# Scaled sums and column sums moved between engines, exponentials in a pool of their own, and the first work of the next stage in another order

## The chip, the core and the metric

The kernel runs on one core of a Trainium2 chip. The metric is the device time of one execution in microseconds (us). An engine is named here as the profile names it: PE is the matrix engine (PEld its weight loads), ACT is ScalarE, DVE is VectorE, POOL is GpSimd, SP is SyncE, which only issues transfers. The queues of ACT and SP both carry DMA issues.

## The reference

The input `x` is 4 images of 128 channels and 64 x 64 points, in float32. Two layers follow one another.

```python
# layer 0: convolutions of 7x7, 5x5 and 3x3 and a full attention over the 4096 points of an image
v = gn(x)
x7, x5, x3 = conv2d(v, w7, b7, 3), conv2d(v, w5, b5, 2), conv2d(v, w3, b3, 1)
f = einsum('bcn,bcm->bnm', theta(v), phi(v)) / sqrt(64)
xn = conv1x1(einsum('bcm,bnm->bcn', g(v), softmax(f)), ow, ob) + v
x = x + relu(x7 + x5 + x3 + xn + v)
# layer 1: a two-way Mamba layer over the 4096 tokens of an image, then a recurrence
t = tokens(x)
t = t + mamba(ln(t), fwd) + reverse(mamba(reverse(ln(t)), bwd))
t = t + scan(lambda y, w: sigmoid(w + y @ V.T), batch_norm(ln(t) @ W.T))
```

In `mamba` a token is projected to z, x, B, C and dt; x, B and C pass a causal filter of four taps and a silu; then comes a scan over chunks, whose decays are exponentials of differences of cumulated dt.

## The kernel before

One program holds three stages, `conv_attention` (0 to about 1711 us of the profile), `mamba` and `recurrence`. A fallback in plain forms follows under an `If`, which is not entered with these inputs. The images lie side by side in one tile `t` for the whole program: 128 channels x 4 x 4096 points.

**Steps.** `conv_attention` runs 32 steps: 4 images (b) by 8 (q). A step does two things at once. The first is the attention of 512 query points over the 4096 keys of the image, in 8 iterations of the loop `for i in range(NB)`. An iteration has `scores` for the iteration after it (8 matmuls L453 into `pf`, two exponentials L455 into `ex`) and `values` (8 matmuls L464 from `ex` into `acc`, and two sums of exponentials on DVE into `es`, the first of a step on L468, the others on L470). `ex` is a tag with four buffers, of which an iteration takes two. At the end of the step L639 folds `es`, and `divide` takes its column sums with a matmul (`den`, L474).

The second is one of eight parts, called m, of the joint convolution. All three kernels are summed into one 7x7 kernel, and the rows of the image are convolved in a transformed domain (groups of output rows j = 0 to 3, with transformation points U and V and their squares UU and VV), which needs fewer products. `transform` (L292 to L325) and `forms` (L335 to 344) make the transformed rows `yx`, `yd`, `yf` of part m on ACT and POOL during the attention iterations. `convolve` then runs the products (`products`, L364) between the attention of this step and that of the next. The parts of an image are done in the orders

```python
        FIRST = (6, 7, 1, 2, 0, 5, 3, 4)
        ORDER = (1, 2, 0, 6, 7, 5, 3, 4)
        LAST = (1, 2, 3, 4, 6, 7, 5, 0)
```

for image 0, for images 1 and 2, and for image 3.

**Adding into the image.** Every part's result `eo` has to be added to some of the four output rows j. `put` does that. The first contribution to a place (kept in `begun`) is a copy on POOL, or a multiply on ACT where it is scaled. Later ones are an add on POOL (L387) or, where scaled, two scalar_tensor_tensor on DVE (L390). The parts 1 and 2, and likewise 3 and 4, belong together: sum and difference of the two (L423, L424, L429) go to j = 0, 2 and to j = 1, 3 with factors. These scaled contributions are not put at once. `later` appends them to the list `late`, and one is taken off in each attention iteration of the following step. So they fall in the step after m = 2 and in the step after m = 4. For which of them a place is already begun depends on the order of the parts.

**Weights.** `weights` is a generator that is advanced once per iteration in the first two steps. It sums the three kernels (`sums`, L534), makes sums and differences of the kernel's columns (`thirds`, L542 to L544, in each of the two `SLOT`s), and then the transformed weights (`pair`, L571 to L575, and `store`, L564), which go to DRAM as `wd`. From there `fetch` (L369, on ACT's queue) brings the weights of a part: two of its three tiles in iteration NB-2 of its step, the third in `convolve`. The tag `wt` has two buffers.

**Mamba's start.** `mamba` loads both in-projections (`full_fwd`, `full_bwd`, on SP's queue) and the filter taps (`cw_fwd`, `cw_bwd`, on ACT's), and the scales of the normalization for every token (`tl`, from `first`, on SP's queue). `centre` (L118, L119) takes the mean off the in-projections; `scaled` (L907) multiplies `tl` by the tokens. Then `project_bc`, `project` (L1106 to L1117: the backward x and half of the forward x, a matmul and the filter's taps on ACT and DVE), `project_fwd` (L1097: the other half, filtered in four matmuls), `activate` (silu, L1121) and `differences` (eight subtractions L1150 into `lt`, followed later by an exponential on L1173) prepare the first chunk.

**What sets the order of the work.** On PE and ACT the instructions stand in the order of the program (`manual_schedule`). On DVE, POOL and SP a scheduler orders them from the dependencies and its own estimates, so that the same source line can be placed in front of or behind other work of the step. Tiles are given out by pools: memory of a pool that has been closed is given to a later one, and a load into it waits for the last use of what lay there. The tiles `ex`, `xn` (the normalized image of `keys`) and `es` are in pool `l0_wk`, and so are `eo`, `mid`, `u`, `xr`, `att` and the small ones.

Of the kernel before, what the change touches and what calls it, by code (L numbers as in the profile page):

```python
# [10 lines left out]
F32 = mybir.dt.float32  # L11
AF = mybir.ActivationFunctionType
ALU = mybir.AluOpType
# [140 lines left out]
def conv_attention(nc, tc, k, a, t, B, H, W, flags, load, mem, loads):  # L154
# [32 lines left out]
    with ExitStack() as ctx:  # L187
# [26 lines left out]
        for i, name in enumerate(("b7", "b5", "b3", "ob")):  # L214
            nc.sync.dma_start(bias[:, i : i + 1], a[name])
        nc.gpsimd.memset(xp, 0.0)
        wk = ctx.enter_context(tc.tile_pool(name="l0_wk", bufs=2))
        big = ctx.enter_context(tc.tile_pool(name="l0_big", bufs=1))
        dram = ctx.enter_context(tc.tile_pool(name="l0_dram", bufs=1, space=bass.MemoryType.DRAM))
# [36 lines left out]

        def keys(b, j):

            xn = wk.tile([P, XT // P, P], F32, tag="ex", name="xn", bufs=4)
            nc.vector.tensor_scalar(  # L260
                xn.rearrange("p a l -> p (a l)"), t[:, ds(b * T + j * XT, XT)], *gn[b], ALU.subtract, ALU.mult
            )
            pp = ps_c.tile([P, NC], F32, tag="c", name="pp")
            for e in range(2):
                nc.tensor.matmul(pp[HALF[e]], pw, xn[:, e::2, :], start=True, stop=True)
            n = XT // P
            nc.scalar.activation(
                phi[:, ds(j * n // 2, n // 2), :].rearrange("p a l -> p (a l)"), pp, AF.Identity, bias=pb2
            )
            pg = ps_c.tile([P, NC], F32, tag="c", name="pg")  # L270
            for e in range(2):
                nc.tensor.matmul(pg[HALF[e]], gw, xn[:, e::2, :], start=True, stop=True)
            g = wk.tile([P, NC], F32, tag="row", name="g", bufs=1)
            nc.scalar.copy(g, pg)
            yield
            pt = ps_c.tile([P, n // 2, 2, IC], F32, tag="c", name="gt")
            for i in range(n // 2):
                nc.tensor.transpose(pt[:, i].rearrange("p e c -> p (e c)"), g[:, bass.ts(i, P)], k.ident)
            nc.scalar.copy(gT[:, ds(j * n, n), :], pt.rearrange("p i e c -> p (i e) c"))
# [92 lines left out]
        def convolve(b, m, f, wts):  # L372

            image = t[:, b * T : (b + 1) * T].rearrange("p (k g j c x) -> p g j x k c", g=2, j=4, c=PC, x=2)
            in_ = lambda v: v.rearrange("p x (k c) -> p x k c", c=PC)

            def put(n, j, v, by=1.0):

                out = image[:, n - 1, j]
                if (b, n, j) not in begun:  # L380
                    begun.add((b, n, j))
                    if by == 1.0:
                        nc.gpsimd.tensor_copy(out, v)
                    else:
                        nc.scalar.mul(out, v, by)
                elif by == 1.0:
                    nc.gpsimd.tensor_tensor(out, out, v, ALU.add)  # L387
                else:
                    for x in range(2):
                        nc.vector.scalar_tensor_tensor(out[:, x], v[:, x], by, out[:, x], ALU.mult, ALU.add)  # L390

            by = BY.get(m, 1.0)
            base = None
            for n in range(3):
                if f[n] is None:
                    continue
                fn = [v + (u,) for v, u in zip(f[n], (wts[n], wc) if wts else (wc,))]
                pm = products(fn, (1, 2))
                keep = n and m in (1, 3)
                eo = wk.tile([P, 2, KB // 2 * PC], F32, tag=f"mid{n}" if keep else "eo", name="eo", bufs=1 if keep else 4)  # L400
                nc.scalar.mul(eo[:, 1, :], pm[:, 1, :], by / 2)  # L401
                if wts and n == 1:
                    wts.append(fetch(m, 2))
                for e, op in enumerate((ALU.add, ALU.subtract)):
                    nc.vector.scalar_tensor_tensor(eo[:, e, :], pm[:, 0, :], by / 2, eo[:, 1, :], ALU.mult, op)  # L405
                yield
                pm = products(fn, (0, 3))
                if by == 1.0:
                    nc.vector.tensor_tensor(eo, eo, pm, ALU.add)  # L409
                else:  # L410
                    nc.vector.scalar_tensor_tensor(eo, pm, by, eo, ALU.mult, ALU.add)  # L411
                if n == 0:
                    base = eo
                    yield
                    continue
                if m < 6:
                    nc.gpsimd.tensor_tensor(eo, eo, base, ALU.add)  # L417
                if keep:
                    mid[n] = eo
                elif m == 2:  # L420
                    begun.add((b, n, 0))
                    out = image[:, n - 1, 0]
                    nc.gpsimd.tensor_tensor(out, in_(mid[n]), in_(eo), ALU.add)  # L423
                    nc.gpsimd.tensor_tensor(mid[n], mid[n], eo, ALU.subtract)  # L424
                    for j, v, c in ((2, out, UU), (1, in_(mid[n]), U), (3, in_(mid[n]), U * UU)):
                        later(put, n, j, v, c)
                elif m == 4:
                    u = wk.tile([P, 2, KB // 2 * PC], F32, tag="u", name="u", bufs=2)
                    nc.gpsimd.tensor_tensor(u, mid[n], eo, ALU.add)  # L429
                    nc.gpsimd.tensor_tensor(mid[n], mid[n], eo, ALU.subtract)  # L430
                    put(n, 0, in_(u))
                    for j, v, c in ((2, u, VV), (1, mid[n], V), (3, mid[n], V * VV)):
                        later(put, n, j, in_(v), c)
                else:
                    put(n, {0: 0, 5: 3, 6: 1, 7: 2}[m], in_(eo))
                yield
# [10 lines left out]
        def scores(th, m0):  # L447

            out = []
            for m in range(2 * m0, 2 * m0 + 2):  # L450
                pf = ps_f.tile([P, 2, NC], F32, tag="f", name="pf")
                for e in range(2):
                    nc.tensor.matmul(pf[:, e, :], phi[HALF[e], m, :], th[HALF[e]], start=True, stop=True)  # L453
                ex = wk.tile([P, 2, NC], F32, tag="ex", name="ex", bufs=4)
                nc.scalar.activation(ex, pf, AF.Exp, scale=scale)  # L455
                out.append(ex)
            return out
# [41 lines left out]
        def later(f, *args):  # L499

            late.append(lambda: f(*args))
# [17 lines left out]
        def weights():  # L519
# [18 lines left out]
            def thirds(y0, y1, s):  # L538

                v, new = [w[:, y0:y1, s[i], :] for i in (0, 1, 3)], w[:, y0:y1, s[2], :]  # L540
                ac = free[:, 25 : 25 + y1 - y0, :] if y1 - y0 == 1 else free[:, 0 : y1 - y0, :]
                nc.vector.tensor_tensor(ac, v[0], v[2], ALU.add)  # L542
                nc.gpsimd.tensor_tensor(new, ac, v[1], ALU.subtract)
                nc.vector.tensor_tensor(v[1], ac, v[1], ALU.add)  # L544

            sums(3, 4)

# [65 lines left out]
        for n in range(N):  # L613
# [10 lines left out]
            if more:  # L624
                rows(b + 1, 0, H)
            acc = ps_v.tile([P, NC], F32, tag="v", name="acc")
            es = wk.tile([P, 2, NC], F32, tag="es", name="es", bufs=1)
            for i in range(NB):
                exs = nxt
                if i + 1 < NB:  # L630
                    nxt = scores(th, i + 1)
                values(i, exs, acc, es)
                next(making_forms, None)
                next(making, None)
                if m < 6 and i == NB - 2:
                    wts = [fetch(m, 0), fetch(m, 1)]
                if late:
                    late.pop(0)()
# [231 lines left out]
def mamba(nc, tc, k, a, t, B, T, vec, first=None, after=None, mr=None):  # L870
# [16 lines left out]
    with ExitStack() as ctx:  # L887
# [204 lines left out]
        def project_fwd(gr):  # L1092

            tl, g = gr["tl"], gr["at"][1]
            px = ring.tile([P, MG], F32, tag="big", name="px")
            for tap in range(KC):
                nc.tensor.matmul(px, w[0]["x"][:, tap, :], tl[:, rows(g, 0, tap)], start=(tap == 0), stop=(tap == KC - 1))  # L1097
            nc.scalar.activation(gr["x"][0][:, 0, :], px, AF.Silu, bias=w[0]["cb"][:, 0:1])
# [46 lines left out]
        def differences(m):  # L1145

            for d in range(ND):
                for h in range(NHEAD):
                    v = m["lt"][:, d, h, :]
                    nc.scalar.activation(v, v, AF.Relu, scale=-1.0, bias=m["b"]["cs"][:, d, m["i"], h : h + 1])  # L1150
# [224 lines left out]
        open_step(1)  # L1375
        for act in later:
            act()
        for i, c in STEPS_X:
            project(groups[0], i, c)
        project_fwd(groups[0])  # L1380
        for i, c in STEPS_X:
            activate(groups[0], i, c)
        differences(m[0])
        turn(m[0])
        prepare(m[0])
        differences(m[1])
# [349 lines left out]
```

## Time and profile before

| | us |
|---|---|
| median of 3 runs | 3203.11 |
| lowest and highest run | 3199.3, 3203.25 |
| the profiled execution | 3203.28 |
| its span, first to last instruction | 3201.6 |
| of that, `conv_attention` | about 1711 |
| PE busy | 2957.4 |
| DVE, POOL, ACT busy | 2288.2, 1824.4, 1803.1 |

The mean clock that PE was granted is 0.973 of full speed.

How lines of the profile read: a group is a source line, an engine, an operation, `out<-in` by the names of tiles, shape and count; then the busy time in us and the mean of one in ns; then how long the engine stood idle just before such instructions, and what ended most of that. A line of the waits is the waiting engine and instruction, then `<-` the instruction that released it, and in us the total, the number and the longest. A line of a timeline is the start in us from the beginning of the span, the duration of a run of like instructions, and in brackets the idle time before it. `L` numbers are lines of the kernel before.

### The profile page before, as it was taken

To read this page: it belongs to the slowest core of one execution; us is meant where nothing else is said; L and a number is where in the kernel's file an instruction comes from. 1 tells how busy PE (TensorE), PEld (TensorE's weight loads), DVE (VectorE), ACT (ScalarE), POOL (GpSimd) and SP (SyncE) were. 2 spreads that over 40 slices of the span, in tenths; PEclk is the share of its full clock that TensorE was granted. 3 is DMA by queue.
4 is the path that set the end of the run, shared out by engine and by line. 5 is a ranking of instruction groups with operands and counts; after the bars stand their busy time and mean duration, and the time that the engine had idled before them with its cause. 6 is when DMAs were issued, how large, how long until landed. Compare 5 with 4: busy or idle time off the path is not lost. (4 is left out here: it accounts for less than half of the span.)

```text
span 3201.6 us, 42877 instructions
## 1 busy us (share of the span) xinstructions
PE 2957.4 (92%) x15511; PEld 1463.9 (46%) x15511; DVE 2288.2 (71%) x3476; ACT 1803.1 (56%) x3074; POOL 1824.4 (57%) x1375
## 2 busy tenths in 40 slices
PE   6899999999999999899997899999999999999976
PEld 1344443545444453434443454544444544445445
DVE  6886778767878568687675676767676767777667
ACT  3333434344344334353442887887788778888756
POOL 5166757817668257596073355556655665556644
PEclk9899999999999999999998899999999999999988
DMA  5310010200102001010004233333433444343332
GB/s 190 126 38 30 23 45 23 71 1 23 39 29 66 7 23 38 30 57 30 1 25 130 73 106 107 90 97 84 115 97 93 93 110 97 97 99 93 87 113 107
DMA packets 108393, 224.15 MB, mean 70 GB/s; under 512 B 25678, under 2 KB 29390, under 8 KB 106764
## 3 DMA queue, kind: packets, MB, share of 16 engines
q1 hardware_dynamic: 96588, 177.53, 19.8%
q10 hardware_dynamic: 11584, 43.78, 4.0%
q8 instruction: 125, 2.05, 0.3%
q14 instruction: 96, 0.79, 0.1%
HBM read 200.83 MB, written 20.44 MB: 69 GB/s over the span
## 5 line engine op out<-in xcount | busy, mean ns | idle before, releaser
L470 DVE TENSOR_TENSOR es<-es,ex 128x1024 f32<-128x1024 f32 x448 | 730.5, 1630 | 108.2 <-ACT ex L455 69.5
L455 ACT ACTIVATE ex<-pf 128x1024 f32<-128x1024 f32 x512 | 501.2, 1023 | 479.1 <-PE pf L453 371.8
L453 PE MATMUL pf<-theta,phi 64*128 64x512 f32 x2048 | 524.1, 630 | 49.0 <-ACT ex L455 47.5
L464 PE MATMUL acc<-ex,gT 128*64 128x512 f32 x2048 | 493.5, 608 | 4.5 <-ACT ex L455 4.5
L1184 POOL TENSOR_TENSOR ct<-ct,Cst 128x512 f32<-128x512 f32 x128 | 170.5, 1332 | 397.3 <-DMA ct<-csmem 335.5
L453 PEld LDWEIGHTS pf<-theta,phi 64*128 64x128 f32 x2048 | 175.1, 189 | 374.8 <-ACT ex L455 237.5
L1150 ACT ACTIVATE lt<-lt,cs 128x128 f32<-128x128 f32 x1024 | 312.1, 390 | 0.0
L364 PE MATMUL pm<-yf,wt 128*128 128x256 f32 x1152 | 286.6, 381 | 21.5 <-DMA wt<-wd 20.5
L401 ACT ACTIVATE eo<-pm 128x256 f32<-128x256 f32 x88 | 33.8, 384 | 476.2 <-PE pm L364 461.5
L464 PEld LDWEIGHTS acc<-ex,gT 128*64 128x64 f32 x2048 | 127.7, 137 | 346.0 <-issue 331.7
L364 PEld LDWEIGHTS pm<-yf,wt 128*128 128x128 f32 x1152 | 212.3, 189 | 97.7 <-issue 44.9
L335 POOL TENSOR_TENSOR yf<-yd 128x272 f32<-128x272 f32 x192 | 253.0, 1349 | 0.0
L1085 PE MATMUL pb<-tl,wbc_fwd 128*64 128x512 f32 x512 | 236.0, 604 | 1.9 <-DVE xT L1117 1.9
L1085 PE MATMUL pb<-tl,wbc_bwd 128*64 128x512 f32 x512 | 236.6, 604 | 0.0
L417 POOL TENSOR_TENSOR eo<-eo 128x512 f32<-128x512 f32 x48 | 61.6, 1284 | 272.7 <-DVE eo L411 190.1
L1249 POOL TENSOR_TENSOR yT<-yT,zT 128x512 f32<-128x512 f32 x127 | 168.3, 1334 | 33.7 <-DVE yT L1236 31.4
L1183 DVE TENSOR_TENSOR lt<-lt,gm 128x1024 f32<-128x1024 f32 x128 | 181.7, 1420 | 1.9
L387 POOL TENSOR_TENSOR t<-t,eo 128x512 f32<-128x512 f32 x28 | 38.0, 1356 | 226.9 <-DVE eo L409 225.7
L335 POOL TENSOR_TENSOR yf<-yx 128x272 f32<-128x272 f32 x96 | 149.9, 1590 | 1.9
L1117 DVE SCALAR_TENSOR_TENSOR xT<-px,taps_bwd,xT 128x512 f32<-128x512 f32 x192 | 143.7, 749 | 8.1 <-ACT xT L1111 3.3
L1216 PE MATMUL y<-lt,xdt 128*64 128x128 f32 x2048 | 141.8, 281 | 7.8 <-PE ptr L1159 4.0
L405 DVE SCALAR_TENSOR_TENSOR eo<-pm,eo 128x256 f32<-128x256 f32 x176 | 73.5, 418 | 101.4 <-ACT eo L401 99.2
(295 smaller groups left out, 5794.3 us busy)
## 6 DMA issues: line engine op xcount, KB each, us to landing
lt<-csmem SPq DMA_DIRECT2D x128, 512.0 KB, 5.6
wt<-wd ACTq DMA_DIRECT2D x72, 576.0 KB, 3.8
ct<-csmem SPq DMA_DIRECT2D x256, 128.0 KB, 5.3
rs<-m SPq DMA_DIRECT2D x31, 512.0 KB, 3.8
wd<-t SPq DMA_DIRECT2D x16, 576.0 KB, 2.8
t<-in_x SPq DMA_DIRECT2D x4, 2048.0 KB
rows<-after SPq DMA_DIRECT2D x32, 256.0 KB, 4.5
out<-t SPq DMA_DIRECT2D x4, 2048.0 KB, 14.4
```

Of the source, the lines that this page charges most:

```text
L335: nc.gpsimd.tensor_tensor(f[:, kx], at(x), at(y), op)
L364: nc.tensor.matmul(pm[:, e, :], wt, src, start=(i == 0), stop=(i == len(terms) - 1))
L453: nc.tensor.matmul(pf[:, e, :], phi[HALF[e], m, :], th[HALF[e]], start=True, stop=True)
L455: nc.scalar.activation(ex, pf, AF.Exp, scale=scale)
L464: nc.tensor.matmul(acc[HALF[e]], gT[:, 2 * m + e, :], ex[:, e, :], start=(m == 0), stop=(m == NT // 2 - 1))
L470: nc.vector.tensor_tensor(es, es, ex, ALU.add)
L1085: nc.tensor.matmul(out, w[i]["bc"][:, tap, bass.ts(c, DS)], src, start=(tap == 0), stop=(tap == KC - 1),)
L1117: nc.vector.scalar_tensor_tensor(at(n), px, taps[:, PAD - n : KC - n], at(n), ALU.mult, ALU.add)
L1150: nc.scalar.activation(v, v, AF.Relu, scale=-1.0, bias=m["b"]["cs"][:, d, m["i"], h : h + 1])
L1183: nc.vector.tensor_tensor(lt, lt, gm.unsqueeze(2).to_broadcast([P, ND, NHEAD, P]), ALU.mult)
L1184: nc.gpsimd.tensor_tensor(m["ct"], m["ct"], Cs[:, cols].unsqueeze(1).to_broadcast([P, NHEAD, P]), ALU.mult)
L1249: eng.tensor_tensor(v, v, gr["z"][d][:, :, half(d, j // 2)], ALU.mult)
```

## The change

Five things differ.

1. `ex`, `xn` and `es` get a pool of their own, `l0_ex`, opened before `l0_wk`. The memory that `mamba` gives to the in-projections and the taps is then that of the exponentials.
2. In `put`, a scaled contribution is multiplied on ACT: into the image where it is the first, else into a tile. That tile is a spare of tag `xr` (two buffers), or, for j = 3, the result itself in place. The add is one instruction on POOL. The scheduled contributions are appended by the new `put_middle`, in the same order j = 2, 1, 3.
3. The two DVE sums of `thirds` go to POOL, where the third operation already was.
4. The first two weights of a part are fetched in iteration NB-3 instead of NB-2.
5. At Mamba's start `project_fwd` comes before the `project`s, and `differences` between these and `activate`. The same order is in the fallback.

The line numbers of the new kernel are higher by 2 from L216 on and by 5 from about L430 on.

```diff
+        ep = ctx.enter_context(tc.tile_pool(name="l0_ex", bufs=4))
         wk = ctx.enter_context(tc.tile_pool(name="l0_wk", bufs=2))
...
-            xn = wk.tile([P, XT // P, P], F32, tag="ex", name="xn", bufs=4)
+            xn = ep.tile([P, XT // P, P], F32, tag="ex", name="xn")
...
-            def put(n, j, v, by=1.0):
+            def put(n, j, v, by=1.0, own=None):
 
                 out = image[:, n - 1, j]
-                if (b, n, j) not in begun:
-                    begun.add((b, n, j))
-                    if by == 1.0:
-                        nc.gpsimd.tensor_copy(out, v)
-                    else:
-                        nc.scalar.mul(out, v, by)
+                if by != 1.0:
+                    to = out if (b, n, j) not in begun else in_(own)
+                    nc.scalar.mul(to, v, by)
+                    v = to
+                if (b, n, j) in begun:
+                    nc.gpsimd.tensor_tensor(out, out, v, ALU.add)
                 elif by == 1.0:
-                    nc.gpsimd.tensor_tensor(out, out, v, ALU.add)
-                else:
-                    for x in range(2):
-                        nc.vector.scalar_tensor_tensor(out[:, x], v[:, x], by, out[:, x], ALU.mult, ALU.add)
+                    nc.gpsimd.tensor_copy(out, v)
+                begun.add((b, n, j))
+
+            def put_middle(n, u, v, at):
+
+                spare = lambda: wk.tile([P, 2, KB // 2 * PC], F32, tag="xr", name="sc")
+                later(lambda: put(n, 2, u, at * at, spare() if (b, n, 2) in begun else None))
+                later(lambda: put(n, 1, in_(v), at, spare() if (b, n, 1) in begun else None))
+                later(lambda: put(n, 3, in_(v), at * at * at, v))
...
-                    for j, v, c in ((2, out, UU), (1, in_(mid[n]), U), (3, in_(mid[n]), U * UU)):
-                        later(put, n, j, v, c)
+                    put_middle(n, out, mid[n], U)
...
-                    for j, v, c in ((2, u, VV), (1, mid[n], V), (3, mid[n], V * VV)):
-                        later(put, n, j, in_(v), c)
+                    put_middle(n, in_(u), mid[n], V)
...
-                ex = wk.tile([P, 2, NC], F32, tag="ex", name="ex", bufs=4)
+                ex = ep.tile([P, 2, NC], F32, tag="ex", name="ex")
...
-                nc.vector.tensor_tensor(ac, v[0], v[2], ALU.add)
+                nc.gpsimd.tensor_tensor(ac, v[0], v[2], ALU.add)
                 nc.gpsimd.tensor_tensor(new, ac, v[1], ALU.subtract)
-                nc.vector.tensor_tensor(v[1], ac, v[1], ALU.add)
+                nc.gpsimd.tensor_tensor(v[1], ac, v[1], ALU.add)
...
-            es = wk.tile([P, 2, NC], F32, tag="es", name="es", bufs=1)
+            es = ep.tile([P, 2, NC], F32, tag="es", name="es", bufs=1)
...
-                if m < 6 and i == NB - 2:
+                if m < 6 and i == NB - 3:
                     wts = [fetch(m, 0), fetch(m, 1)]
...
+        project_fwd(groups[0])
         for i, c in STEPS_X:
             project(groups[0], i, c)
-        project_fwd(groups[0])
+        differences(m[0])
         for i, c in STEPS_X:
             activate(groups[0], i, c)
-        differences(m[0])
```

## The prediction

> **What bounds the kernel now.** I read the page's busy shares first, then its costliest groups, then the waits of the convolution and attention stage (0 to 1720 us), then engine timelines around the largest waits.
>
> ```profile
> PE 2957.4 (92%) x15511; PEld 1463.9 (46%) x15511; DVE 2288.2 (71%) x3476; ACT 1803.1 (56%) x3074; POOL 1824.4 (57%) x1375
> L455 ACT ACTIVATE ex<-pf 128x1024 f32<-128x1024 f32 x512 | 501.2, 1023 | 479.1 <-PE pf L453 371.8
> L470 DVE TENSOR_TENSOR es<-es,ex 128x1024 f32<-128x1024 f32 x448 | 730.5, 1630 | 108.2 <-ACT ex L455 69.5
> ```
>
> PE is the bound: a saving counts only where PE stands. In an iteration of attention the PE timeline shows 1.99 us of scores (L453) and 1.94 of values (L464), a period of 3.78; ScalarE needs 1.94 of it for two exponentials, 1.84 is spare. The waits say where PE stands:
>
> ```profile
> PE pf L453 <- ACT ex L455: 47.5, 42, 6.6
> ACT ex L455 <- DVE es L470: 57.7, 41, 10.1
> ACT ex L455 <- DVE es L468: 41.9, 6, 9.0
> PE pm L364 <- DMA wt<-wd: 20.5, 28, 3.5
> PE den L474 <- DVE es L639: 11.6, 6, 7.7
> ```
>
> Six waits behind DVE's first sum of exponentials (L468) cost ScalarE 41.9 us. DVE's and ScalarE's timelines at such a place, the first step of image 1:
>
> ```profile
> 484.99 1.86 DVE L390 SCALAR_TENSOR_TENSOR t<-u,t 128x256 f32<-128x256 f32 x2 [2.73 <-POOL u L429]
> 486.77 7.11 DVE L390 SCALAR_TENSOR_TENSOR t<-eo,t 128x256 f32<-128x256 f32 x4
> 493.81 1.21 DVE L468 TENSOR_TENSOR es<-ex 128x1024 f32<-128x1024 f32 x1
> ```
> ```profile
> 495.12 1.94 ACT L455 ACTIVATE ex<-pf 128x1024 f32<-128x1024 f32 x2 [7.48 <-DVE es L468]
> ```
>
> The scaled sums (L390) stand ahead of `es`, so the `ex` buffers stay taken, ScalarE waits 7.48 and PE 5.51. By step, PE waits for `ex` 5.39 us at step 4 (image 0), 5.78, 5.84, 5.78, 5.80 at steps 8, 16, 24, 28; elsewhere 0.27 mostly, 14.42 in step 0.
>
> **What the Trainium skill says.** *TensorE: Matmul & The Clock Gate*, "Architectural detail: the array is 16× 32×32, not 1× 128×128", says that ScalarE and VectorE work their queues in strict order: the trace agrees, `es` runs at 493.81 though its data was there at 487.6. *GPSIMD Engine Reference*, "3.1 Elementwise", gives an add of 2048 elements 4497 ns on GpSimd, 2293 on VectorE; the trace has 1356 (L387) against 665 (L409) at 512, the same twofold. The same page's "Specifications" says that GpSimd shares its SBUF interfaces with VectorE instructions of two SBUF inputs. It agrees: L335's 128x272 adds take from 638 ns to a median of 1621, the long ones beside DVE's `es` sums.
>
> **The change, part by part.** All against the profiled execution, 3203.28 us (3201.6 of span, 1.7 around it); the median of the runs is 3203.11, no correction.
>
> *Scaled sums.* 56 L390 instructions (36+16+4 in the groups, 58.6 us) leave DVE. In their place 28 ScalarE multiplies (0.68 each in the ScalarE timeline at 267.59, hidden in the 1.84 spare of an iteration; without it 28 x 0.7 = 20 us) and 28 POOL adds (1.36 by L387).
> Steps 8, 16, 24, 28: the stall goes. A step with the same pair of forms lasts 59.39 where it is stalled and 53.06 where not, so 6.3 per stall of 5.4 (the clock falls a little when PE stands). 4 x 6.2 = **-25**; -23.2 by the waits alone.
> Step 4 is different: two spares serve four scaled sums (tag `xr`, two buffers), so the third multiply waits for the first's add on POOL, and POOL's new order puts all four adds behind step 4's twenty row sums:
>
> ```profile
> 252.76 1.53 POOL L424 TENSOR_TENSOR eo<-eo 128x512 f32<-128x512 f32 x1
> 254.25 2.71 POOL L296 TENSOR_TENSOR yx<-yx,xp 128x1190 f32<-128x1190 f32 x1
> 257.04 2.76 POOL L296 TENSOR_TENSOR yx<-yx,yb 128x1190 f32<-128x1190 f32 x1
> 259.87 5.48 POOL L335 TENSOR_TENSOR yf<-yx 128x272 f32<-128x272 f32 x4
> 265.31 4.27 POOL L344 TENSOR_TENSOR yd<-yx 128x560 f32<-128x560 f32 x2
> 269.54 6.38 POOL L335 TENSOR_TENSOR yf<-yd 128x272 f32<-128x272 f32 x4
> 275.89 6.40 POOL L335 TENSOR_TENSOR yf<-xp 128x272 f32<-128x272 f32 x4
> 282.24 4.89 POOL L335 TENSOR_TENSOR yf<-yd 128x272 f32<-128x272 f32 x4
> ```
>
> These end at 287.1. ScalarE would want the third multiply at about 266.0. Queued behind it are the next exponentials, hence PE, then DVE, which runs dry by 268.5; from there POOL is alone and the last twelve row sums take 0.65 each and `yd` 1.3: rows end at 278.1, the add at 279.4. Exponentials follow at 280.1 instead of 267.9: 12.2 us late, and 2 more for the clock; minus the old stall of 6.3 gives **+7.8**. From +4 (POOL alone from earlier on) to +18 (POOL at its old speed, 288.4).
> In steps 8, 16, 24 POOL's new order has the first scaled add third, behind two transform adds, near 494.8; the multiply waiting for it is wanted near 499. The `mid` tiles that the next form reuses come free at 519.8 and 523.7, wanted at 520.9 and 526.7. No cost, with margins of 4, 1.1 and 3 us.
>
> *Column sums (L542, L544).* Twelve leave DVE (6.5 us busy), for POOL:
>
> ```profile
> 49.91 0.56 DVE L544 TENSOR_TENSOR t<-t 128x384 f32<-128x384 f32 x1 [1.11 <-POOL t L543]
> 50.50 1.36 DVE L571 SCALAR_TENSOR_TENSOR t<-t 128x1152 f32<-128x1152 f32 x1
> 51.78 1.22 DVE L470 TENSOR_TENSOR es<-es,ex 128x1024 f32<-128x1024 f32 x1
> 52.91 1.35 DVE L573 SCALAR_TENSOR_TENSOR t<-t 128x1152 f32<-128x1152 f32 x1
> ```
>
> POOL starts at 35.5: 3 x 0.98 + 6 x 0.46 (128x128, scaled from the others by size) + 12 x 1.0 + the copy 1.4 = 19.1, so the thirds are complete at 54.6, not 50.5. DVE's new order has L571 and L573 ahead of the second `es` sum, which ends at 60.0 instead of 53.0. DVE then has less to do, but POOL's weight sums (L564) and the denominator (L474, wait of 7.7 there) come later by 3 to 6. I take **+6**, from 0 (cover by the 3 us that DVE stands idle at 45 to 50) to +14 (7 twice: exponentials and denominator).
>
> *Fetch one iteration earlier.* Of the 20.5 us on `wt`, 17 waits with 14.4 us are at a form's first weights, 11 with 6.1 at its third, which doesn't move. The largest of the first kind:
>
> ```profile
> 1685.62 1.96 PE L364 MATMUL pm<-yf,wt 128*128 128x256 f32 x8 [3.48 <-DMA wt<-wd]
> ```
>
> The issue moves by 3.78 us, more than any of these waits, on ScalarE's queue in place of one later; the tile comes free at the previous form's end, long before. **-12.5**, from -9 to -14.4.
>
> *Own pool for `ex`, `xn`, `es`.* Mamba's in-projection then lands where the exponentials were, freed near 1688, before it waited for POOL's last sum at 1713.8:
>
> ```profile
> 1717.09 2.49 PE L118 MATMUL centre<-full_fwd,ones 128*128 128x512 f32 x4 [6.72 <-DMA full_fwd<-in_fwd_in_proj]
> 1723.60 2.08 PE L118 MATMUL centre<-full_bwd,ones 128*128 128x512 f32 x2 [4.02 <-DVE full_fwd L119]
> ```
>
> That is not 10.7 us of gain: the first projection also needs `tl`, whose loads wait for the last relu (L516 ends at 1716.02) in both kernels; its last product ends at 1731.76, beside the projection at 1731.81. The loads move 1.67 of 4.08 MB out of the way, so `tl` is ready near 1729.4: **-2.5**, from 0 to -5. By the skill's *TensorE: Matmul & The Clock Gate*, "What's actually happening", an idle PE drops to half clock; here it is at 0.63 from 1710 to 1727 and stays idle, so nothing more comes of it.
>
> *Order at Mamba's start.* In the chain of waits, after the backward projection's sums:
>
> ```profile
> 1752.89 6.66 PE px L1097 x8
> 1760.16 1.66 ACT xT L1121 x3
> 1761.82 2.33 ACT lt L1150 x8
> ```
>
> The forward projection now comes first, and the differences (L1150) lie under the DVE sums instead of behind the activations. The second exponential starts near 1760.6 instead of 1765.46: **-4.5**, from -1 to -6.
>
> Sum: -25 +7.8 +6 -12.5 -2.5 -4.5 = -30.7, so 3203.3 - 30.7, near **3173 us**.
>
> **The rivals.** *A: POOL falls behind at every scaled stage (slower).* The scheduler's order of POOL may not be kept up with: it is at 35.2 of 52 us there, each row sum 1.6 beside DVE. Decides if the first scaled add of steps 8, 16, 24 ends after 499, or a `mid` add far past 520.9. ScalarE then waits as in step 4: 14 each instead of -6.2, three times +20.2 = +60.6 on the sum, **3233**. Against it: only two transform adds (some 6 us) lie ahead.
> *B: the losses take most of the gain.* Step 4 at POOL's old speed (+18), column sums +14, fetch -10, the rest -3 with -23: -4, **3199**, the same within the 0.2% (6.4 us) that a measurement of this kernel can tell. For it: POOL's 128x272 adds are slow wherever DVE runs.
> *C: the fetch wait is only moved.* If `wt` comes when the queue allows, the PE's wait goes to `yf` from POOL (0.9 us in that group now): **3186**.
> *D: step 4 costs only its +4*, as POOL speeds up earlier: -34.5, **3169**.
>
> **How the numbers follow.** My sum has 0.60 with D's side in it, C 0.17, B 0.13, A 0.06, and 0.04 for mishaps unlisted. The bounds added up are 3156 and 3199. Taken as independent, they spread the sum by some 9 us, and with C the middle 8 in 10 reach from 3158 to 3193. Chances: all of the sum and C, and a quarter of B, are faster than 3196.7: 0.84; within 6.4 us 0.09; slower 0.07 (A, and part of the unlisted).
>
> **What would show it.** Right: in steps 8, 16, 24, 28 the L468 waits of ScalarE are gone and PE's wait for `ex` falls from 5.8 to below 1; in step 4 a multiply (new L384) waits for POOL some 12 us and PE with it; PE's `wt` waits fall from 20.5 to about 7; DVE's second `es` sum in step 0 ends near 60; the first centre matmul no longer waits for its load; the forward px precede the backward ones. Wrong: a multiply waiting on POOL in steps 8, 16 or 24 (A), step 0 longer by over 14 us, `wt` waits unchanged.

## The result, and the profile after

The changed kernel takes 3199.59 us (median of 4 runs, 3199.33 to 3204.35); the kernel before, on the same chip, 3202.62 (4 runs). The ratio is 0.9996 with a 95% interval of 0.9979 to 1.0013: no difference that can be measured. The forecast was 3173 with a range of 3158 to 3193. The profiled execution after took 3199.33 us with a span of 3197.6, 4.0 below the span of before.

First the page's busy shares and the group of the sums of exponentials (the one of the exponentials themselves has the same mean of 1023 ns as before):

```profile
PE 2953.9 (92%) x15511; PEld 1463.8 (46%) x15511; DVE 2263.5 (71%) x3408; ACT 1817.2 (57%) x3102; POOL 1875.5 (59%) x1415
L475 DVE TENSOR_TENSOR es<-es,ex 128x1024 f32<-128x1024 f32 x448 | 767.3, 1713 | 121.6 <-ACT ex L460 82.5
```

The scaled sums and the column sums left VectorE (56 and 12 instructions), yet it was busy for only 25 us less in all, because the 448 sums of exponentials, which the change doesn't touch, took 767.3 us instead of 730.5. Then the waits of the convolution and attention stage, in the same form as before (waiting instruction, releaser, total, times, longest):

```profile
PE pf L458 <- ACT ex L460: 44.5, 44, 12.4
PE den L479 <- DVE es L644: 22.1, 10, 9.7
DVE t L491 <- POOL t L387: 21.4, 3, 7.2
ACT sc L384 <- POOL t L387: 15.9, 2, 14.7
PE pm L366 <- DVE t L491: 12.9, 3, 4.8
PE pm L366 <- DMA wt<-wd: 4.4, 9, 1.6
```

Three of these waits did not exist before: VectorE at L491 for GpSimd's adds, PE at L366 for L491, and ScalarE's multiply for GpSimd's adds. The wait for weights fell from 20.5 to 4.4. Where the time went is seen step by step. The table has the interval from the matmul of the queries (L442 before, L447 after) of a step to that of the next one, in us:

| interval | before | after | forecast of the difference | measured |
|---|---|---|---|---|
| start to step 0 | 31.45 | 33.45 | 0 | +2.00 |
| steps 0 to 3 | 207.39 | 208.59 | +6, less a part of the fetch | +1.20 |
| step 4 | 59.39 | 66.15 | +7.8 | +6.76 |
| steps 8, 16, 24 | 57.83, 58.20, 58.08 | 61.68, 61.97, 61.95 | -6.2 each | +3.85, +3.77, +3.87 |
| step 28 | 54.76 | 47.61 | -6.2 | -7.15 |
| all other steps before 31 | | | the fetch | -3.87 |
| step 31 to the first dt matmul (L1005, L1010) | 96.53 | 92.90 | -6 (fetch, own pool) | -3.63 |
| from there to the second group of bc projections | 41.53 | 32.90 | -4.5 | -8.63 |
| the rest | | | 0 | -2.11 |

These add up to -3.94. The first two rows are not independent: with the column sums on GpSimd, step 0 took 78.3 to 78.7 us in the traces in which it began at 31.2 to 31.5 us, and 75.5 to 77.1 where it began at 33.0 to 33.6, so that a part of a later start is won back in it. The one forecast with the wrong sign is that of steps 8, 16 and 24: forecast -18.6, measured +11.5, a miss of 30.1 us, while the whole forecast missed by some 27. Step 8 on VectorE before (L470 are the sums of exponentials, L486 the sum in `collect`):

```profile
495.13 24.48 DVE L470 TENSOR_TENSOR es<-es,ex 128x1024 f32<-128x1024 f32 x14
...
521.83 0.68 DVE L486 TENSOR_TENSOR t<-t,pc 128x512 f32<-128x512 f32 x1
```

Step 8 in the timelines of after, VectorE first, then GpSimd, then PE:

```profile
494.63 30.61 DVE L475 TENSOR_TENSOR es<-es,ex 128x1024 f32<-128x1024 f32 x14 [1.66 <-ACT ex L460]
...
534.24 0.69 DVE L491 TENSOR_TENSOR t<-t,pc 128x512 f32<-128x512 f32 x1 [7.15 <-POOL t L387]
534.84 3.35 DVE L481 RECIPROCAL att<-den 128x512 f32<-128x512 f32 x1
```
```profile
520.95 8.28 POOL L337 TENSOR_TENSOR yf<-yd 128x272 f32<-128x272 f32 x8
529.19 1.29 POOL L387 TENSOR_TENSOR t<-t,eo 128x512 f32<-128x512 f32 x1
530.43 2.53 POOL L387 TENSOR_TENSOR t<-t,sc 128x512 f32<-128x512 f32 x2
532.92 1.29 POOL L387 TENSOR_TENSOR t<-t,eo 128x512 f32<-128x512 f32 x1
```
```profile
526.35 1.12 PE L479 MATMUL den<-es,ones 128*128 128x512 f32 x2 [2.43 <-DVE es L644]
534.98 3.50 PE L366 MATMUL pm<-yf,wt 128*128 128x256 f32 x8 [4.85 <-DVE t L491]
```

L491 is the sum in `collect`: it adds the last attention result of the image before into `t`, the same image into which GpSimd still puts the last four scaled contributions, behind its row sums. VectorE takes its queue in order: the reciprocal behind L491 starts at 534.84, though the denominator that it reads was done at 527.47. The sums of the products behind it stand as well. PE stands with them, since the matmul that waits needs a PSUM tile of the same tag as the `pc` that L491 has yet to read. So the traces show one wait that was not there before. The first line of VectorE holds a second possible cause: 14 sums of exponentials took 30.61 us, where in step 8 of before they took 24.48. They ended late, and PE waited 2.43 us for the denominator and 1.86 for exponentials.

### The profile page after: what moved, and what is told of

Same layout as the page of the kernel before. It is cut to its first block, busy times and chain, and to the rows that moved or that the text cites. A ratio compares the mean times of both kernels' runs of the same rounds, so it can differ in the third digit from the quotient of the medians.

```text
span 3197.6 us, 42890 instructions
## 1 busy us (share of the span) xinstructions
PE 2953.9 (92%) x15511; PEld 1463.8 (46%) x15511; DVE 2263.5 (71%) x3408; ACT 1817.2 (57%) x3102; POOL 1875.5 (59%) x1415
## 5 line engine op out<-in xcount | busy, mean ns | idle before, releaser
L475 DVE TENSOR_TENSOR es<-es,ex 128x1024 f32<-128x1024 f32 x448 | 767.3, 1713 | 121.6 <-ACT ex L460 82.5
L460 ACT ACTIVATE ex<-pf 128x1024 f32<-128x1024 f32 x512 | 502.0, 1023 | 436.9 <-PE pf L458 356.4
L366 PE MATMUL pm<-yf,wt 128*128 128x256 f32 x1152 | 294.5, 389 | 17.3 <-DVE t L491 12.9
L366 PEld LDWEIGHTS pm<-yf,wt 128*128 128x128 f32 x1152 | 217.1, 193 | 95.2 <-issue 40.8
L337 POOL TENSOR_TENSOR yf<-yd 128x272 f32<-128x272 f32 x192 | 242.0, 1291 | 0.0
L387 POOL TENSOR_TENSOR t<-t,eo 128x512 f32<-128x512 f32 x36 | 50.2, 1394 | 202.5 <-DVE eo L416 201.2
L337 POOL TENSOR_TENSOR yf<-yx 128x272 f32<-128x272 f32 x96 | 151.3, 1604 | 1.6
## 6 DMA issues: line engine op xcount, KB each, us to landing
t<-in_x SPq DMA_DIRECT2D x4, 2048.0 KB, 10.9
```

The source lines that it names most:

```text
L337: nc.gpsimd.tensor_tensor(f[:, kx], at(x), at(y), op)
L366: nc.tensor.matmul(pm[:, e, :], wt, src, start=(i == 0), stop=(i == len(terms) - 1))
L475: nc.vector.tensor_tensor(es, es, ex, ALU.add)
```

## The experiments

**Theory 1**: the loss in steps 8, 16 and 24 is the wait at L491. **Theory 2**: it is GpSimd's adds running beside VectorE's sums of exponentials, and the wait at L491 only shows what would be lost anyway. The medians of the kernel before in the sets below lie between 3203.7 and 3205.6.

**L491 later.**

```diff
-                    if q not in ((1, 2, 3) if b == 0 else (1,)):
+                    held = sorted(atts) if q == 0 else []
+                    if q and q not in ((1, 2, 3) if b == 0 else (1,)):
...
+                if i == 2:
+                    for o in held:
+                        collect(o, atts.pop(o))
```

> The changed kernel, but in the first step of an image the attention sum of the image before (L491) is made two groups of products later. Theory 1: in steps 8, 16 and 24 VectorE's queue stands at L491, which waits for GpSimd's last scaled adds into the same image; with L491 later, PE no longer waits for it (4.85, 3.18, 4.85 us in the changed kernel), and the three steps fall from 61.7, 62.0, 62.0 us to 56 or 57, so the time falls by 13 to 18 us, to about 3184. Theory 2: the loss comes from GpSimd's adds slowing VectorE's sums of exponentials beside them, and the wait at L491 only shows it; then the steps stay at 60 or more and the time above 3195.

Measured: 3186.69 us, ratio to before 0.9952 (0.9935 to 0.9968). The three steps took 57.61, 57.61 and 57.64 us, so 4.1 to 4.4 less. The wait at L491 is gone, as theory 1 has it, but the steps are still 6 us above the forecast of 51.6. PE in step 8:

```profile
525.47 1.12 PE L479 MATMUL den<-es,ones 128*128 128x512 f32 x2 [3.28 <-DVE es L644]
```

The 14 sums of exponentials are as slow as without the edit (30.59 us), and PE waits for the denominator instead. So theory 1 explains 4.3 us of a miss of 10.3 in a step, and no more. Some 1.7 us of the 57.6 are the clock's: right after this wait PE was granted 0.51 of full speed from 526.8 to 530.3, and likewise in the other two steps (step 8 of the changed kernel has such a stretch too, so its 4.1 compare like with like). In steps 8 and 24 of the first mended version below, where the same instructions meet no such stretch, the steps take 55.96 and 56.05.

**Without the scaled adds.**

```diff
                 if (b, n, j) in begun:
-                    nc.gpsimd.tensor_tensor(out, out, v, ALU.add)
+                    if by == 1.0:
+                        nc.gpsimd.tensor_tensor(out, out, v, ALU.add)
```

> The changed kernel without GpSimd's adds of scaled sums to places already begun (ScalarE's multiplies stay), so these contributions are missing from the output. If only these adds cost what was lost, by whichever of the two ways, steps 8, 16 and 24 fall to the 51.5 us that were forecast and step 4 loses its stall of 12.3 us: about 45 us less than the changed kernel, near 3155. If ScalarE's multiplies or something else has a part in it, the three steps stay above 54 us.

Measured: 3160.26 us in one run. Steps 8, 16, 24: 53.81, 53.80, 53.81; step 4: 52.18. So 8.1 of the 10.3 us go with the adds, whatever their way, and 2.2 do not. VectorE in step 8, all 14 sums first, then two single ones of them:

```profile
481.20 29.30 DVE L476 TENSOR_TENSOR es<-es,ex 128x1024 f32<-128x1024 f32 x14 [1.66 <-ACT ex L461]
```
```profile
486.56 3.36 DVE L476 TENSOR_TENSOR es<-es,ex 128x1024 f32<-128x1024 f32 x1
...
504.26 1.49 DVE L476 TENSOR_TENSOR es<-es,ex 128x1024 f32<-128x1024 f32 x1
```

With VectorE no longer held up by L390, its sums start earlier in the step and run beside GpSimd's work from first to last, one every 2.09 us on the mean, where they took 1.75 before. What a sum takes depends on what GpSimd does beside it. The 3.36 us are beside a transform add (L298, 128x1190, on GpSimd from 485.33 to 488.83), the 1.49 beside row sums (L337, 128x272, from 503.04). Before, the first two of the three transform adds ran while VectorE was still at L390, so that only one of its sums met one (499.11, 3.55 us). PE waits in this step for 1.81 us for the denominator and 1.24 for exponentials, so the trace puts the 2.2 us that are left on the slower sums; no run leaves out the transform adds, or ScalarE's multiplies, to show it.

**The scaled adds first**, three contributions per iteration and ahead of the form:

```diff
-                next(making_forms, None)
-                next(making, None)
...
-                if late:
-                    late.pop(0)()
+                for _ in late[: 3 if scaled else 1]:
+                    late.pop(0)()
+                next(making_forms, None)
+                next(making, None)
```

> The changed kernel, but in steps 8, 16 and 24 the late contributions are taken off the list three per iteration and ahead of the making of the form, so that in GpSimd's order all six scaled adds stand before the row sums. Theory 1 (only L491's wait counts): the wait goes as in the run with the later L491, steps of 57.6 us again or less, 3186. Theory 2 (contention has the larger part): VectorE's sums of exponentials still run beside GpSimd throughout, and GpSimd's row sums end 5 us later, so PE waits for them and the steps stay above 59 us.

Measured: 3198.6 us, ratio 0.998 (0.997 to 0.999); steps of 60.28, 60.82, 61.22. That looks like theory 2, but the trace has another reason, in ScalarE's timeline:

```profile
504.33 0.63 ACT L384 ACTIVATE sc<-u 128x512 f32<-128x512 f32 x1 [5.47 <-POOL t L387]
```

A multiply waits for its spare, which is the mechanism of step 4 brought into step 8. The run is inconclusive on the two theories. It was made again with two more spares:

```diff
-                spare = lambda: wk.tile([P, 2, KB // 2 * PC], F32, tag="xr", name="sc")
+                tag, bufs = ("att", 4) if at == V and n == 2 else ("xr", 2)
+                spare = lambda: wk.tile([P, 2, KB // 2 * PC], F32, tag=tag, name="sc", bufs=bufs)
```

> The run with the scaled adds first, where ScalarE's fourth multiply waited 5.5 us for a spare, so that it decided nothing; now with two more spares (tag att, free at that place), so that no multiply waits. Neither L491 nor a spare waits for GpSimd's adds then, but all six adds still run beside VectorE's sums of exponentials. If waits were the loss (theory 1), steps 8, 16 and 24 fall to 53.8 us, as in the run without the adds. If GpSimd's adds cost by running beside VectorE (theory 2), they stay at 57.6, where the later L491 left them, or above 56.

Measured: 3191.37 us in one run, steps of 57.18, 57.20, 57.17. No multiply and no sum in `collect` waits for GpSimd in step 8. VectorE there, all sums and a single one of them, and GpSimd:

```profile
495.57 32.13 DVE L476 TENSOR_TENSOR es<-es,ex 128x1024 f32<-128x1024 f32 x14 [1.66 <-ACT ex L461]
```
```profile
508.85 2.13 DVE L476 TENSOR_TENSOR es<-es,ex 128x1024 f32<-128x1024 f32 x1
```
```profile
503.15 4.51 POOL L387 TENSOR_TENSOR t<-t,sc 128x512 f32<-128x512 f32 x2
```

The adds take 2.26 us each beside the sums of exponentials, where they take 1.29 alone; a sum beside them takes 2.13. The step is 3.4 us longer than without the adds, and VectorE accounts for it: 2.83 us in the 14 sums and 0.53 in L646, which folds them (1.55 against 1.02). Neither trace has a stretch of lower clock in step 8. That is theory 2's number, without the waits of theory 1. The two theories hold side by side: of the 10.3 us of a step 4.3 are the wait and 3.4 the adds beside VectorE (with L491 later 3.8, of which 1.7 are the clock's), and 2.2 are left without any add.

**The scaled sums back on VectorE.** `put` and its callers as before, all else as changed.

```diff
-                    put_middle(n, in_(u), mid[n], V)
+                    for j, v, c in ((2, u, VV), (1, mid[n], V), (3, mid[n], V * VV)):
+                        later(put, n, j, in_(v), c)
```

> The changed kernel with the scaled sums as before, on VectorE; the other parts of the change stay. Both theories: steps 8, 16, 24 go back to 57.8 to 58.2 us, step 4 to about 58, step 28 to 54.8; that is 11 us less than the changed kernel, near 3188. If the parts of the change are not independent (the earlier fetch or the own pool depend on the scaled sums), it is off by more than 4 us.

Measured: 3189.98 us, ratio 0.996 (0.9945 to 0.9974); step 4 59.37, steps 8, 16, 24 59.02, 58.03, 58.01, step 28 54.44. So the move of the scaled sums, by itself, costs some 10 us (10.5 by these five steps), and the other parts of the change gain some 14.

**Four spares in step 4.**

```diff
-                spare = lambda: wk.tile([P, 2, KB // 2 * PC], F32, tag="xr", name="sc")
+                tag = "u" if at == U and n == 2 else "xr"
+                spare = lambda: wk.tile([P, 2, KB // 2 * PC], F32, tag=tag, name="sc", bufs=2)
```

> The changed kernel with four spare tiles in step 4 of image 0 (the two of tag u, not yet in use there, beside the two of xr). If the third multiply waits for nothing but its spare, PE's wait of 12.3 us in step 4 goes and the time falls by 12 to 14 us, to about 3186. Rival: GpSimd's four adds, which now end later than the multiplies, hold up L491 or the next form instead, and no more than 5 us are gained.

Measured: 3199.34 us (12 runs, 3190.79 to 3201.47), ratio to before 0.9984 (0.9976 to 0.9993), where the changed kernel has 0.9996 (0.9979 to 1.0013): a gain of 4 us at most is left, and the intervals overlap. In the profiled execution, one of the fastest with 3191.4, step 4 fell from 66.15 to 61.72. The rival held. VectorE in step 4:

```profile
293.18 1.88 DVE L492 TENSOR_TENSOR t<-t,pc 128x512 f32<-128x512 f32 x3 [7.14 <-POOL t L387]
```

The line is `collect` again (L492 in this kernel). Behind the multiply's wait lay the same wait as in step 8.

**Column sums on VectorE, fetch in NB-2, the old pool, the old order**: each undoes one part.

```diff
-                nc.gpsimd.tensor_tensor(ac, v[0], v[2], ALU.add)
+                nc.vector.tensor_tensor(ac, v[0], v[2], ALU.add)
...
-                nc.gpsimd.tensor_tensor(v[1], ac, v[1], ALU.add)
+                nc.vector.tensor_tensor(v[1], ac, v[1], ALU.add)
```

> The changed kernel with the column sums as before on VectorE. By the forecast steps 0 and 1 together get shorter by 6 us, the stall of 12.4 us at the second pair of exponentials going back to 6.6. Rival: the shorter work of VectorE later in step 0 had paid part of it back, and no more than 3 us are gained.

Measured: 3200.56 us in one run. Step 0 ends 2.4 us earlier than in the changed kernel, but at the start of step 4 only 0.7 is left (241.33 against 242.04 us). So no more than 3 us are gained, as the rival has it, but not for its reason: the 1.7 us between the two figures are lost in step 2 (45.25 us against 43.59), where this trace has a stretch of lower clock (0.57 from 189 to 193 us). Against the traces of other runs that began about as early, at 31.2 to 31.5 us, step 0 ends 3.1 to 3.7 us earlier. Step 0 still takes 74.85 us, not the 71.16 of before; the rest of that difference was not traced further.

```diff
-                if m < 6 and i == NB - 3:
+                if m < 6 and i == NB - 2:
```

> The changed kernel with the first two weights fetched in iteration NB-2 as before. By the forecast PE's waits for weights rise from 8 to about 20 us and the time by 12.5 us. Rival (the wait is only moved): PE then waits elsewhere instead, and the sum over the undisturbed steps and the last convolution grows by 8 us or less, 3.5 of it in the last one.

Measured: 3213.62 us in one run. PE's waits for weights in the first 1730 us rose to

```profile
PE pm L366 <- DMA wt<-wd: 21.2, 28, 3.2
```

and PE reached the first matmul of `centre` at 1728.05 instead of 1717.11 us, 10.9 later. Not all of that is the fetch's: from the queries of step 31 to the end of the last relu this run takes 82.27 us, the changed kernel 76.23, and the kernel before, which fetches as late, 79.75. This run's last convolution has a clock of 0.54 from 1699 to 1706.5 us. Between the traces of before and after, the two rows that hold the fetch gave 3.9 and 3.6. So it is worth 7 to 11 us, less than the forecast 12.5.

```diff
-        ep = ctx.enter_context(tc.tile_pool(name="l0_ex", bufs=4))
...
-                ex = ep.tile([P, 2, NC], F32, tag="ex", name="ex")
+                ex = wk.tile([P, 2, NC], F32, tag="ex", name="ex", bufs=4)
```

(`xn` and `es` likewise.)

> The changed kernel with ex, xn and es back in the pool that they were in. Theory: the early loads of the in-projections are hidden by the chain over tl, so that the time from the last relu (L521) to the first dt matmul stays at 16.7 us and nothing is lost. By the forecast this stretch gets 2.5 us longer. Rival: without the early loads the loads of tl come later as well, and the stretch grows by 5 us or more.

Measured: 3204.12 us in one run. From the end of the last relu (1725.31) to the first dt matmul (1743.54) 18.2 us, where the changed kernel has 16.7 (16.0 to 16.8 in the other traces with the same code there): the pool is worth 1.6. Before it was 16.8, so against the kernel before the stretch gained nothing.

```diff
-        project_fwd(groups[0])
         for i, c in STEPS_X:
             project(groups[0], i, c)
-        differences(m[0])
+        project_fwd(groups[0])
         for i, c in STEPS_X:
             activate(groups[0], i, c)
+        differences(m[0])
```

> The changed kernel with the order at Mamba's start as before. By the forecast the stretch from the first cumulated sum (L1049) to the second group of bc projections (23.7 us in the changed kernel, 32.3 before) gets longer by 4.5 us; if the whole difference of the two traces there is this order's, by 8.6 us.

Measured: 3204.18 us in one run. The stretch took 28.4 us against 23.7: 4.7 for the order. The other 3.9 to the 32.3 of before are not the order's. 2.9 of them are in one line of the chain, the four-tap projection, which read 6.66 us before and here

```profile
1761.65 3.72 PE px L1102 x8
```

the same eight matmuls, at a granted clock of 1.00 where before it was 0.57 (from 1752 to 1760 us).

**The out-projection's scaling on ScalarE**, to see why the own pool returned so little:

```diff
-                    nc.gpsimd.tensor_scalar(out[:, c, :], out[:, c, :], vec["nw_" + d][:, c : c + 1], None, ALU.mult)
+                    nc.scalar.mul(out[:, c, :], out[:, c, :], vec["nw_" + d][:, c : c + 1])
```

> The changed kernel with the scaling of the out-projection (L969) on ScalarE instead of GpSimd. Theory: GpSimd's last two products into tl stand behind these four, which wait for a load that is now issued later, and that is why the early in-projections return nothing: with them gone the stretch from the last relu to the first dt matmul falls from 16.7 us by 2 to 4. Rival: tl's own loads set its end (VectorE waits for them until 1733.2); then less than 1 us.

GpSimd in the changed kernel, and then in this one:

```profile
1732.43 1.20 POOL L969 TENSOR_SCALAR wout_fwd<-wout_fwd,nw_fwd 128x128 f32<-128x128 f32 x2 [5.23 <-DMA wout_fwd<-in_fwd_out_proj]
...
1736.54 1.09 POOL L912 TENSOR_TENSOR tl<-tl,t 128x512 f32<-128x512 f32 x1
```
```profile
1732.40 1.09 POOL L912 TENSOR_TENSOR tl<-tl,t 128x512 f32<-128x512 f32 x1 [1.72 <-DMA tl<-first]
```

The stretch from the last relu (1724.00) to the first dt matmul (1736.25) fell to 12.3 us from 16.7, so 4.4, a little over the 2 to 4 expected (in the mended versions below the same edit takes 2.5 off, from 16.4 to 13.9); the run took 3194.56. In the changed kernel ScalarE issues the out-projection's load at 1724.85, behind copies that now come before it, 2 us after the relu; before it was issued at 1717.06, 1 us after. GpSimd then waits for that load, and the products into `tl` behind it.

**The mended versions.** L491 later in step 4 as well, four spares there, column sums on VectorE:

> All mended: L491 later in steps 8, 16, 24 and in step 4 (the sums of steps 0 to 2 are then made in step 3), four spares in step 4, column sums on VectorE. If theory 1 holds and the parts add up: -12.7 as with L491 later, -10 in step 4 (66.2 to about 56), -3 for the column sums, so 3199 - 26 = about 3173. If contention carries the rest of step 4 as well, it stays near 61 us there and the time near 3180.

Measured: 3172.86 us, ratio 0.9901 (0.9885 to 0.9918). Step 4 took 50.78 us, better than the 56 expected and than the 59.39 of before. 2.7 us of that are only moved: step 3, which now makes the sums of steps 0 to 2, took 48.89 instead of 46.19. With both waits gone the stall is away: in step 4 PE waits for the denominator for 1.43 us and for exponentials for 0.27, where in the changed kernel it waited for exponentials for 12.31. With the scaling of the out-projection on ScalarE in addition:

> The run with L491 later, the spares and the column sums on VectorE, with the scaling of the out-projection on ScalarE too. If the parts add up it is 2 to 4 us below that run, near 3170; else the same, 3173.

Measured: 3170.01 us (4 runs, 3168.43 to 3174.09), ratio 0.9895 (0.9878 to 0.9911): some 1% faster than both kernels. Its interval and that of the version without the last edit overlap. With the scaled adds first as well:

> All mended (L491 later, column sums on VectorE, out-projection on ScalarE), with the scaled adds first and four spares in steps 8, 16 and 24 as well. Theory 1: three steps of 53.8 instead of 56 to 57.6, 8 to 10 us less, near 3161. Theory 2: no gain, 3170.

Measured: 3176.18 us, ratio 0.99 (0.9884 to 0.9917); steps 8, 16, 24 took 59.45, 59.71, 60.76 instead of 57.63, 55.96, 57.73, and no multiply waits for a spare there. No gain, as theory 2 has it; that it is even slower in these steps was not taken apart, and some of it is the clock's (0.5 for 3.4 us in step 8 and for 6.8 in the other two, towards their ends).

## Why the prediction was wrong

The failed step is this one of *Scaled sums*: "4 x 6.2 = -25", with "No cost, with margins of 4, 1.1 and 3 us" for steps 8, 16 and 24.

- **Steps 8, 16, 24**: -6.2 each forecast, +3.8 to +3.9 measured. The prediction asked who waits for GpSimd's new adds and followed ScalarE's multiplies and the `mid` tiles. It didn't ask who else touches what the adds write. That is the image, and VectorE's sum in `collect` writes the same one. Before, both stood on VectorE and their order cost no wait (L486 at 521.83). That accounts for 4.3 us a step (shown by the run with L491 later). Nor did it price the adds on the engine that they run beside: 3.4 us (shown by the two runs with and without them in which nothing waits for the adds). The prediction had quoted the slow GpSimd adds as a cost to GpSimd; it put VectorE's side at nothing without a reason, though it had named the shared interface. And 2.2 us are the measure of the gain: it took over the 6.3 us between two other steps (4 and 10), and freeing VectorE earlier put its sums beside the transform adds. This last part is read from the traces and not shown by a run of its own.
- **Step 28**: -6.2 forecast, -7.2 measured. There the form needs no transform, and GpSimd is done with its row sums early: its last scaled add ends at 1550.65, before VectorE's sums do (1554.40). These are slower there too, 1.88 us each on the mean against 1.22 before, but PE waits only 0.29 us for the denominator, and L491 not at all.
- **Step 4**: +7.8 forecast, +6.8 measured. The multiply waited 14.71 us and PE 12.04; 12.2 was forecast for the lateness. The waits lay as told, GpSimd's speeding up when VectorE runs dry included (the row sums ended at 280.9, forecast 278.1). It was not told that the wait of the sum in `collect` is right behind (the run with four spares).

```profile
282.21 0.67 ACT L384 ACTIVATE sc<-t 128x512 f32<-128x512 f32 x1 [14.71 <-POOL t L387]
```

- **Column sums**: +6 forecast, +0.7 by undoing them, up to the start of step 4; +2.4 at the end of step 0. The mechanism was right: VectorE's second `es` sum ended at 60.3 (60.0 forecast), with VectorE waiting for the last third:

```profile
55.23 2.63 DVE L576 SCALAR_TENSOR_TENSOR t<-t 128x1152 f32<-128x1152 f32 x2 [14.94 <-POOL t L549]
```

 The size was off: step 0 pays part of the delay back. The rest of the difference between 2.4 and 0.7 is a stretch of lower clock in the run that undid them.
- **Fetch**: -12.5 forecast, -10.9 by undoing it, some 7 between the traces of before and after. A part of the wait moved on: PE now waits for VectorE's products (1.84 us each at the denominator of steps 10, 18 and 26), where rival C had named GpSimd's `yf`.
- **Own pool**: -2.5 forecast, -1.6 measured by undoing it. That `tl` sets the end was right. What held `tl` was not its loads alone but GpSimd's queue.
- **Order at Mamba's start**: -4.5 forecast, -4.7 measured.

The parts as measured are 11.5 - 7.2 + 6.8 + 0.7 - 10.9 - 1.6 - 4.7 = -5.4, against -4.0 between the two traces. That they come so near is luck in part: the fetch and the column sums are uncertain by 2 to 4 us each, and the start, Mamba's clock and the rest of the kernel (+2.0, -3.9, -2.1) stand outside the sum. The time is that of rival B (3199), but not for its reasons: of its terms only the fetch (-10) came near; step 4 and the column sums cost less than forecast, and the gain of the scaled sums, which it kept at -23, did not come. Rival A named the right three steps and the right engine, with the wrong waiter.

Two sums of the prediction are slightly off, and nothing hangs on them: the ends of its ranges add up to 3157 and 3200 rather than 3156 and 3199, and the parts that it names for faster (all of the sum and C, a quarter of B) make 0.80, not 0.84.

## What to carry to other kernels

When an operation moves to another engine, list everyone who reads or writes the place that it writes, not only who feeds it: an order that one queue kept for nothing becomes a wait on the engine that stayed. Then price what the moved work does to the engine that it runs beside, in that engine's own instructions, and look at what else those instructions will now run beside. And where a wait is taken away, look for the next one on the same place before its time is counted as gained: in steps 3 and 4 together it took the later `collect` and the spares, 112.3 to 99.7 us, where the spares alone gave 108.1.

## What the hardware showed that was not expected

How much VectorE's sums of two SBUF inputs and GpSimd's adds slow each other went beyond what the prediction had used. The same 128x1024 sum took 1.22 us with GpSimd idle, 1.48 beside its 128x272 row sums, 2.13 beside its 128x512 adds and 3.33 to 3.56 beside its 128x1190 transform adds. GpSimd's row sum went from 0.65 to 1.57, its 128x512 add from 1.29 to 2.26; its transform add took 3.50 there and 2.49 at the least. So the longer GpSimd's instruction, the more a sum beside it takes: for the row sums and the 128x512 adds 0.83 to 0.84 us more than the GpSimd instruction takes by itself. The Trainium skill says in *GPSIMD Engine Reference*, "1. Specifications", that the two share their SBUF interfaces in such instructions; the runs agree, and show that both sides pay, and how much.

The start of the kernel, which the edits do not touch, took 30.8 to 33.6 us to the first queries in the traces. In the one of 33.5 (after) the first four PE matmuls of the second key block still took 1.97 us, in the one of 31.5 (before) 1.08; the speed of 1.08 was there some 5 us later. From the second group of bc projections to its end the kernel took 1420.6 to 1428.5 us in the traces, again without an edit that touches it. Both are as large as several of the terms above, and are why these were read from steps and not from totals. Single steps scatter too: one stretch of 3.4 us at half clock in a step is 1.7 us.
